# A second level of the seven-product form in the down product of a gated FFN with a long convolution

## The chip, the cores and the metric

The kernel runs on one core of one Trainium2 chip. The metric is the device time of one execution in microseconds. A core has the engines TensorE (PE, matrix products, with its weight loads shown apart as PEld), VectorE (DVE), ScalarE (ACT), GpSimd (POOL) and SyncE (SP). In this kernel SP and POOL mainly issue DMA transfers; the transfers themselves are done by 16 DMA engines of the core.

## The reference, cut to what matters

For 2048 tokens of 1024 features the reference computes, in float32,

```python
xn = layernorm(x)
y  = causal_convolution(xn, K) + D[0] * xn       # along the 1024 features, K (1024 entries) from the S4 parameters
h  = silu(xn @ Wg.T) * (xn @ Wu.T)               # 2752 inner entries, int4 weights, groups of 64
out = x + y + h @ Wd.T                           # Wd int4 as well, 1024 x 2752
```

Two products dominate: gate and up (2048 x 1024 by 1024 x 5504) and down (2048 x 2752 by 2752 x 1024). The convolution runs along each token's 1024 features and is a triangular Toeplitz product. The int4 weights have to be unpacked, scaled and shifted before use.

## The kernel before

A float32 product is made of three float16 products: each operand is split into a hi and a lo float16 part (hi is a rounded copy, made on ACT; lo is operand minus hi, made on DVE), and hi·hi + hi·lo + lo·hi is summed in PSUM. So each 128 x 128 weight block costs three weight loads and three matmuls (the loops over `PASS`).

Both large products use one level of the Winograd form of the 2 x 2 block product: seven block products P1 to P7 of sums of blocks (factors) in place of eight. `PROD` names, for each product, the factor of either side.

Phase A makes gate and up for 21 i tiles of 128 inner entries (and a half tile), j = 0 to 20, over two pairs of token chunks (`cp` = 0, 1; a chunk is 512 tokens). For each j, `load_w` (L351) turns two packed granules into split factors: `unpack` on DVE, 16 scaling ACTIVATEs on ACT, four sums on DVE, a hi copy on ACT, a lo subtraction on DVE (`factors`, L305), and a transposing DMA into a `wf` tile. `gate_up` (L411) then issues 84 matmuls and its evacuations. `finish_h` (L465) waits for two i tiles, forms the seven sums of h, splits each into hi and lo, and stores them to DRAM (`HSP`). Beside this, at ten values of j (`WD_AT`, L45), `load_wd` (L366) unpacks two granules of the down weights, forms and splits the seven factors and stores them (`WDN`). At six further places `keep_x` stores blocks of x for the convolution, and L507 to L624 compute the convolution's kernel.

Phase B makes the down product over ten pairs of i tiles. For each of the two `cp` and seven products, `load_factor` (L823) brings split factors back, weights through a transposing DMA (`wd`) and h plainly (`hd`), all through the SP queue. `product` (L844) issues 30 matmuls of 512 columns per 128 tokens: h is the stationary operand, the weights the moving one. `rest` (L854) adds, in the same PSUM bank, the convolution and the last one and a half i tiles; `common` (L879) makes a part of the convolution in another bank. `finish` (L888) loads x, adds the partial results to it on DVE and stores the output. The sums U2 and U3 are kept in `h` tiles of 512 columns.

What sets the order: every engine runs its instructions in one fixed order, written when the kernel is built. Only the first part of phase A (L630 to L699) and the steps around `pinned` have an order written by hand. Elsewhere the framework's scheduler orders them by program priority and its own timeline (L1044). A tile that reuses a buffer makes its first writer wait for the last user. So a DMA issued by SP or POOL that waits for a buffer, or for data, holds up all that stands behind it in that queue.

The tile pools that matter here: `u8` (14 buffers of 8 KB per partition for x blocks, inputs, and later `wd` and `hd`), `h` (10 of 2 KB), `hf` (3), `nat` (2), `wf` (4), the dequantized granule `w` (2), and 8 PSUM banks.

## Time and profile before

| | |
|---|---|
| three runs | 1349.52, 1351.09, 1357.06 us; median 1351.09 us |
| profiled execution | span 1353.8 us. Of the three times shown only 1357.06 us is not below that span, so only that one can be the profiled execution's own; 3.3 us would then lie around the span |
| TensorE busy | 1304.3 us, 96% of the span, granted clock 0.991 |
| VectorE, ScalarE, GpSimd busy | 791.9 us (58%), 630.2 us (47%), 211.8 us (16%) |
| phase A on TensorE | until 856.5 us |
| phase B on TensorE | 856.5 to 1350.1 us: 1680 matmuls of `product`, and 832 of `rest` and `common` |
| DMA | 242.7 MB, 179 GB/s over the span; 65% of the DMA engines' time on SP's queues, 4.5% on POOL's |

How to read it: busy time is the union of an engine's instruction spans. Matmuls are pipelined, so the mean of one (380 ns for 512 columns) is a latency; what a matmul costs in a stream is the distance between starts. An idle time is put down to the event that ended it. Most vector and scalar instructions carry the line of a helper (L79 or L84), so groups are told apart by the names of their operands. A DMA's time to landing counts from its issue.

### The profile page before, as it was taken

The page shows a single profiled execution, that of the slowest core. Times are in us where ns is not written, and L with a number is a line of the kernel's source. Part 1 is how long each engine was busy: PE and PEld are TensorE (multiplying, and loading weights), DVE is VectorE, ACT ScalarE, POOL GpSimd, SP SyncE. Part 2 cuts the span into 40 slices and gives each one's busy share as a digit, 9 for nine tenths or more (in the row PEclk, how much of TensorE's full clock was granted, in tenths as well). Part 3 has the DMA queues.
Part 4 walks back from the last instruction along what each step waited for, and adds up shares of the span by engine and source line. Part 5 has one row for each costly group of instructions (what it writes and reads, how often), then busy time and mean ns, then how long its engine had stood idle before and what let it go on. Part 6 is the DMA issues. An engine that isn't in the chain of part 4 may idle for free.

```text
span 1353.8 us, 17402 instructions
## 1 busy us (share of the span) xinstructions
PE 1304.3 (96%) x6404; PEld 614.2 (45%) x6404; DVE 791.9 (58%) x1303; ACT 630.2 (47%) x1374; POOL 211.8 (16%) x354
## 2 busy tenths in 40 slices
PE   2798999999999999999999999989999999999998
PEld 2343444444444444444444444434444554444464
DVE  7679998788798878997887865241111412111131
ACT  5478378697896676879988872100000000000000
POOL 5235042221321121212242300000000000000000
PEclk9899999999999999999999999999999999999999
DMA  8994728557466656665866668999878759767420
GB/s 228 232 199 107 171 68 188 128 144 191 122 183 155 183 166 159 198 192 170 211 177 158 176 124 227 264 305 268 203 199 220 225 176 255 199 162 203 124 86 24
DMA packets 400370, 242.70 MB, mean 179 GB/s; under 512 B 338132, under 2 KB 358556, under 8 KB 396444
## 3 DMA queue, kind: packets, MB, share of 16 engines
q1 hardware_dynamic: 394012, 225.98, 64.7%
q0 software_dynamic: 6272, 15.60, 4.5%
q8 instruction: 50, 0.82, 0.2%
q14 instruction: 36, 0.29, 0.1%
HBM read 83.47 MB, written 74.45 MB: 117 GB/s over the span
## 4 chain that ended last, share of the span: by engine, by line
PE 64%; DMA 4%; DVE 2%; SPq 1%; issue 1%; ACT 1%; DVEq 0%; ACTq 0%
PE o L848 25%; PE C L418 9%; PE D L418 9%; PE A L418 8%; PE B L418 4%; PE o L876 4%; PE o L859 2%; DMA wf<-nat 2%; SPq L79 1%; DMA hd<-HSP 1%; PE o L867 1%; PE c L884 1%; PE o L871 1%; PE o L861 1%; PE o L860 1%
## 5 line engine op out<-in xcount | busy, mean ns | idle before, releaser
L418 PEld LDWEIGHTS <-wf 128*128 128x128 f16 x3192 | 312.8, 98 | 386.4 <-issue 11.8
L848 PE MATMUL o<-wd,hd 128*128 128x512 f16 x1680 | 368.3, 380 | 4.0 <-DMA hd<-HSP 4.0
L79 ACT ACTIVATE w<-w,sc 128x64 f32<-128x64 int32 x960 | 326.8, 427 | 65.3 <-DVE w L79 62.6
L848 PEld LDWEIGHTS <-hd 128*128 128x128 f16 x1680 | 163.7, 98 | 197.5 <-DMA hd<-HSP 4.5
L418 PE MATMUL C<-x,wf 128*128 128x512 f16 x912 | 211.9, 382 | 3.7 <-DVE u L79 3.7
L418 PE MATMUL A<-x,wf 128*128 128x512 f16 x912 | 211.3, 380 | 3.0 <-DMA wf<-nat 2.4
L418 PE MATMUL D<-x,wf 128*128 128x512 f16 x912 | 209.2, 379 | 0.0
L79 DVE TENSOR_TENSOR nat<-w,nat 128x1792 f16<-128x1792 f32 x58 | 117.0, 2019 | 24.4 <-ACT nat L79 24.2
L79 ACT COPY v<-o 128x512 f32<-128x512 f32 x8 | 4.7, 585 | 268.5 <-PE o L848 268.5
L79 DVE TENSOR_TENSOR w<-w 128x256 f32<-128x256 f32 x232 | 97.0, 419 | 48.5 <-ACT w L79 46.4
L79 ACT CAST nat<-w 128x1792 f16<-128x1792 f32 x58 | 97.3, 1678 | 35.0 <-DMA wf<-nat 29.2
L418 PE MATMUL B<-x,wf 128*128 128x512 f16 x456 | 107.5, 382 | 0.0
L390 PEld LDWEIGHTS <-wf 128*128 128x128 f16 x624 | 56.7, 104 | 91.3 <-DMA wf<-natp 30.5
L79 DVE TENSOR_TENSOR v<-o,v 128x512 f32<-128x512 f32 x24 | 16.6, 691 | 138.8 <-PE o L848 138.8
L79 DVE SCALAR_TENSOR_TENSOR o<-o,o 128x512 f32<-128x512 f32 x32 | 22.0, 688 | 125.5 <-PE o L876 125.3
L283 POOL TENSOR_SCALAR sc<-sz 128x16 f32<-128x16 f32 x61 | 49.0, 803 | 233.8 <-ACT w L79 225.2
L255 POOL DMA_DIRECT2D raw<-in_raw x56 | 32.5, 581 | 267.2 <-DVE w L79 252.5
L390 PE MATMUL g<-x,wf 128*128 128x512 f16 (+1 forms) x264 | 48.1, 341 | 27.2 <-DMA wf<-natp 24.9
L79 DVE SCALAR_TENSOR_TENSOR o<-v,o 128x512 f32<-128x512 f32 x32 | 21.9, 691 | 77.3 <-DMA o<-in_x 57.7
L876 PE MATMUL o<-band,xc 128*128 128x512 f16 (+3 forms) x384 | 57.5, 300 | 0.0
L79 DVE TENSOR_TENSOR hf<-ha,hf 128x512 f16<-128x512 f32 x72 | 48.9, 685 | 13.3 <-ACT hf L79 13.2
L79 ACT CAST hf<-ha 128x512 f16<-128x512 f32 x72 | 43.5, 612 | 23.5 <-DVE ha L79 18.0
(132 smaller groups left out, 1097.9 us busy)
## 6 DMA issues: line engine op xcount, KB each, us to landing
HSP<-hf SPq DMA_DIRECT2D x60, 512.0 KB, 3.6
hd<-HSP SPq DMA_DIRECT2D x28, 768.0 KB, 5.3
WDN<-nat SPq DMA_DIRECT2D x20, 896.0 KB, 4.6
raw<-in_raw POOLq DMA_DIRECT2D x56, 256.0 KB, 4.1
hd<-HSP SPq DMA_DIRECT2D x14, 1024.0 KB, 5.6
n<-in_xp SPq DMA_DIRECT2D x16, 512.0 KB, 4.8
XSP<-x SPq DMA_DIRECT2D x8, 1024.0 KB, 5.8
xc<-XSP SPq DMA_DIRECT2D x8, 1024.0 KB, 7.1
```

Of the source, the lines that this page charges most:

```text
L79: return method(*args, **kw)
L255: ld.dma_start(raw, raw_d[gi].rearrange("p (a b) -> p a b", a=16))
L283: G.tensor_scalar(sc[:, 0], sz[:, 0], WS, None, ALU.mult)
L390: PE.matmul(ps[:, ts], w(k, wi), xt[k // 4][:, xi, k % 4, ts], start=(k == 0 and n == 0), stop=(k == 7 and n == 2))
L418: PE.matmul(ps, wf[kt // 2][:, 4 * fa + 2 * wi + kt % 2, :], xt[:, xi, kt, :], start=(start and kt == 0 and n == 0), stop=(stop and kt == ...
L848: PE.matmul(ps.rearrange("p (a b) -> p a b", a=2), hh[gi][:, n, hi, q * P : (q + 1) * P], wd[gi][:, n, :, wi, :], start=(g0 + n == 0 and k ...
L859: PE.matmul(ps, hpl[:, c, hi, ts], wp[:, 0, wi, cols], start=False, stop=False, skip_group_check=again)
L860: PE.matmul(ps, hpl[:, c, 2, ts], wp[:, 1, 0, cols], start=False, stop=False, skip_group_check=again)
L861: PE.matmul(ps, hpl[0:64, c, 2, ts], wp[0:64, 1, 1, cols], start=False, stop=False, skip_group_check=again)
L867: PE.matmul(ps[:, 0:256], xt[:, xi, k + 2, ts], diff[:, bi, P - P * k : P - P * k + 256], start=False, stop=False, skip_group_check=again)
L871: PE.matmul(ps[:, 256:512], xt[:, xi, k, ts], diff[:, bi, 512 - P * k : 768 - P * k], start=False, stop=False, skip_group_check=again)
L876: PE.matmul(ps[:, P * k : 512], xt[:, xi, k, ts], band[:, bi, 0 : 512 - P * k], start=False, stop=(k == 3 and n == 2), skip_group_check=again)
```

## The change

The down product gets a second level of the same form. Each of the seven outer products (k) is itself a 2 x 2 block product, over the token halves (`cp`), the two halves of the ten pairs of i tiles, and alternate tiles of 128 hidden entries; it is made of seven inner products (m). An inner product is 60 matmuls of 256 columns: two halves `qq` of 256 tokens, two tiles of 128 tokens, five pairs of i tiles, three passes. The 49 items (k, m) follow one another, with the next k's first item moved ahead of the last two of this k.

In phase A, `finish_h` stores the seven sums of h unsplit as float32 (`HF`), one DMA each. `load_wd` handles two granules from the two halves of the pairs at once, makes the second-level factors (four more subtractions on half tiles), and stores each of the seven inner factors of either kind apart (`WD2`). Only one of the four blocks of x is stored for the convolution; the other three stay in SBUF.

In the last phase, `load_a` brings h sums back through POOL's queue, `operands` makes the second-level sums of h on DVE and splits them on ACT and DVE (`gsplit`), and `load_b` brings the weights through a transposing DMA on SP. `prepare` runs four items ahead; there are five `g` buffers and five for b. Accumulators U and W stay in SBUF. `result` loads a partial output through POOL, adds to it and stores it.

The convolution and the last i tiles become a stage between the two (`conv`), with PSUM banks of their own. Its sum with x goes to DRAM (`PART`), and `result` reads it back. `add_split` makes its hi copy on ACT rather than DVE. The pools are laid out anew: x blocks live in `ux` (6) and `ut` (8, shared with the inputs), `h` has 12 buffers, and the pools of the last phase take the place of those of phase A tile by tile.

```diff
-        u8 = pool("u8", bufs=14)
-        hp_ = pool("h", bufs=10)
-        hfp = pool("hf", bufs=3)
+        hp_ = pool("h", bufs=12)
...
-        XSP = [[dr.tile([P, 2, 4, 512], F16, name=f"XSP{c}{f}") for f in range(4)] for c in range(2)]
-        HSP = [dr.tile([7, P, NPAIR, 1024], F16, name=f"HSP{c}") for c in range(2)]
+        XSP = [dr.tile([P, 2, 4, 512], F16, name=f"XSP{c}") for c in range(2)]
...
-        WDN = dr.tile([7, P, NPAIR, 1024], F16, name="WDN")
+        WD2 = [dr.tile([7, P, NPAIR // 2, 2, 2, P], F16, name=f"WD{m}") for m in range(1, 8)]
+        PART = [[dr.tile([1024, 512], F32, name=f"PART{c}{h}") for h in range(2)] for c in range(2)]
...
+        ea = ExitStack()
+        right = lambda name, **k: ea.enter_context(tc.tile_pool(name=name, side="right", **k))
+        uxp = pool("ux", bufs=6, side="right")
+        utp = right("ut", bufs=8)
+        wfp = right("wf", bufs=4)
+        natp = right("nat", bufs=2)
+        dqp = right("dq", bufs=2)
+        early = ExitStack()
+        left = ExitStack()
+        right2 = lambda name, **k: left.enter_context(tc.tile_pool(name=name, reuse_waits="tile", **k))
+        hfp = early.enter_context(tc.tile_pool(name="hf", bufs=2))
...
+                home, tag = (uxp, "ux") if f in (0, 1, 3) else (utp, "ut")
+                xf[cp, f] = home.tile([P, 2, 4, 512], F16, tag=tag, name=f"x{cp}_{f}")
...
-            def load_wd(p):
+            def load_wd(u):
+                pr, kq = divmod(u, 2)
+                gs = [G_WD + 2 * p + kq for p in (pr, pr + NPAIR // 2)]
+                ws = []
+                for gi, home in zip(gs, (wxp, dqp)):
+                    w = dequant(gi, home=home)
+                    sums(w, True)
+                    ws.append(w.rearrange("p f (m c) -> p f m c", m=2))
+                wa, wb = ws
+                tt, sub = V.tensor_tensor, ALU.subtract
+                def put(w, ms, products):
+                    nat = natp.tile([P, 7, 2, 2, P], F16, tag="nat", name=f"nd{u}_{products[0]}")
+                    split(nat[:, :, ms].rearrange("p f m a c -> p a f m c"), w[:, :, ms])
+                    for m, i in zip(range(2)[ms], products):
+                        SP.dma_start(
+                            WD2[i - 1][:, :, pr, kq].rearrange("f p a c -> p f (a c)"),
+                            nat[:, :, m].rearrange("p f a c -> p f (a c)"),
+                        )
+                put(wa, slice(0, 1), (1,))
+                tt(wa[:, :, 0], wa[:, :, 1], wa[:, :, 0], sub)
+                tt(wa[:, :, 1], wb[:, :, 1], wa[:, :, 1], sub)
+                put(wb, slice(0, 2), (2, 3))
+                tt(wb[:, :, 1], wb[:, :, 1], wa[:, :, 0], sub)
+                tt(wb[:, :, 0], wb[:, :, 0], wb[:, :, 1], sub)
+                put(wa, slice(0, 2), (5, 7))
+                put(wb, slice(0, 2), (4, 6))
...
-                def emit(f0, srcs):
-                    pc = piece(f"hf{nm}_{f0}")
-                    for i, s in enumerate(srcs):
-                        split(pc[:, i], s)
-                    n = len(srcs)
-                    SP.dma_start(
-                        HSP[cp][f0 : f0 + n, :, pr, :].rearrange("f p c -> p f c"),
-                        pc[:, :n].rearrange("p f a b -> p f (a b)"),
-                    )
-                emit(0, (s0, s1))
...
+                def emit(f, src):
+                    SP.dma_start(HF[cp][f, :, j // 2, :], src)
+                s4, s5, s6 = (htile(f"s{n}_{nm}") for n in (4, 5, 6))
+                emit(0, s0)
+                emit(1, s1)
+                emit(3, s3)
                 V.tensor_tensor(s4, s0, s2, ALU.subtract)
+                emit(4, s4)
                 V.tensor_tensor(s2, s2, s3, ALU.add)
-                V.tensor_tensor(s0, s2, s0, ALU.subtract)
-                V.tensor_tensor(s1, s1, s0, ALU.subtract)
-                emit(5, (s0, s1))
-                emit(2, (s2, s3))
...
+                V.tensor_tensor(s5, s2, s0, ALU.subtract)
+                emit(5, s5)
+                V.tensor_tensor(s6, s1, s5, ALU.subtract)
+                emit(6, s6)
...
+            early.close()
+            wxp = right2("wx", bufs=1)
...
-                if j in XS_AT:
-                    keep_x(*divmod(XS_ORDER[j - XS_AT[0]], 4))
...
+        poolb = lambda name, **k: es.enter_context(tc.tile_pool(name=name, reuse_waits="tile", **k))
+        fp = poolb("f", bufs=6, side="right")
+        gp = poolb("g", bufs=5, side="right")
+        bep = poolb("be", bufs=3, side="right")
+        cvp = poolb("cv", bufs=1)
+        half = NPAIR // 2
...
+        def gtile(name):
+            return gp.tile([P, half, 2, 512], F16, tag="g", name=name)
+        def load_a(k, r, c):
+            t = fp.tile([P, half, 512], F32, tag="f", name=f"a{k}_{r}{c}")
+            G.dma_start(t, HF[r][PROD[k][0], :, half * c : half * c + half, :])
+            fac[r, c] = t
...
+        def load_b(k, m, n):
+            home, tag = (bep, "be") if n % 5 < 3 else (uxp, "ux")
+            t = home.tile([P, half, 2, 2, P], F16, tag=tag, name=f"b{k}_{m}")
+            SP.dma_start_transpose(
+                t.rearrange("p a b c d -> p (a b c) d"), WD2[m - 1][PROD[k][1]].rearrange("p a b c d -> p (a b c d)")
+            )
+            return t
+        def gsplit(src, name):
+            g = gtile(name)
+            A.copy(g[:, :, 0], src)
+            V.tensor_tensor(g[:, :, 1], src, g[:, :, 0], ALU.subtract)
+            return g
+        def operands(k, m, n):
+            tt, sub, add = V.tensor_tensor, ALU.subtract, ALU.add
+            if m == 1:
+                load_a(k, 0, 0)
+                src = fac[0, 0]
+            elif m == 2:
+                load_a(k, 0, 1)
+                src = fac[0, 1]
+            elif m == 6:
+                load_a(k, 1, 0)
+                load_a(k, 1, 1)
+                s1 = fac["s1"] = fp.tile([P, half, 512], F32, tag="f", name=f"s{k}")
+                tt(s1, fac[1, 0], fac[1, 1], add)
+                tt(fac[1, 0], fac[0, 0], fac[1, 0], sub)
+                tt(fac[0, 0], s1, fac[0, 0], sub)
+                fac["s2"] = src = fac[0, 0]
+                fac["s3"] = fac[1, 0]
+                fac["a12"], fac["a22"] = fac[0, 1], fac[1, 1]
+            elif m == 5:
+                src = fac["s1"]
+            elif m == 7:
+                src = fac["s3"]
+            elif m == 4:
+                src = fac["a22"]
+            else:
+                src = fac["a12"]
+                tt(src, src, fac["s2"], sub)
+            b = load_b(k, m, n)
+            return gsplit(src, f"g{k}_{m}"), b
...
+        def conv(cp, c, hh, hpl, xc, xs):
+            for q in range(4):
+                ts = slice(q * P, (q + 1) * P)
+                cols = slice(512 * hh, 512 * hh + 512)
+                ps = bank(f"cv{cp}{c}{hh}{q}")
...
+                for hi, wi in PASS:
+                    mm(ps, hpl[:, c, hi, ts], wp[:, 0, wi, cols])
+                mm(ps, hpl[:, c, 2, ts], wp[:, 1, 0, cols])
+                mm(ps, hpl[0:64, c, 2, ts], wp[0:64, 1, 1, cols], stop=True)
+                t0 = 1024 * cp + 512 * c + P * q
+                o = htile(f"p{cp}{c}{hh}{q}")
+                SP.dma_start(o, x[t0 : t0 + P, cols])
+                V.scalar_tensor_tensor(o, ps, osc, o, ALU.mult, ALU.add)
+                if hh:
...
+                SP.dma_start(PART[cp][hh][512 * c + P * q : 512 * c + P * q + P, :], o)
+        items = [(k, m) for k in SEQ for m in (1, 2, 6, 5, 7, 4, 3)]
+        for n in range(0, len(items) - 7, 7):
+            items[n + 5 : n + 8] = [items[n + 7]] + items[n + 5 : n + 7]
+        ready = []
+        def prepare():
+            n = len(ready)
+            if n < len(items):
+                ready.append(operands(*items[n], n))
...
+        for cp in range(2):
+            hpl = gp.tile([P, 2, 3, 512], F16, tag="g", name=f"hpl{cp}")
             SP.dma_start(hpl, HPL[cp])
-            xc = []
+            x7 = fp.tile([P, 2, 4, 512], F16, tag="f", name=f"x7_{cp}")
+            SP.dma_start(x7, XSP[cp])
+            xc = [xf[cp, 3], xf[cp, 1], x7, xf[cp, 0]]
+            xs = fp.tile([P, 2, 2, 2, 512], F16, tag="f", name=f"xs{cp}")
...
-                wd, hh = load_factor(cp, i)
...
-                    product(ps, wd, hh, q, i not in REST or i == 5)
-                    if i in REST and i != 5:
-                        rest(ps, hpl, xc, *REST[i], q)
...
+            for c, hh in ((0, 0), (1, 0), (0, 1), (1, 1)):
+                conv(cp, c, hh, hpl, xc, xs)
+                if cp:
+                    prepare()
...
+        U = [uxp.tile([P, 4, 512], F32, tag="ux", name=f"U{cp}") for cp in range(2)]
+        W = [uxp.tile([P, 4, 512], F32, tag="ux", name=f"W{cp}") for cp in range(2)]
...
+        banks, zs = {}, {}
+        def matmuls(k, m, qq):
+            g, b = ops
+            new = m in (1, 2, 5)
+            key = {1: "A", 6: "A", 7: "A", 4: "A", 2: "E", 5: "D", 3: "D"}[m]
+            if new:
+                banks[k, key, qq] = bank(f"{key}{k}_{qq}")
+            ps = banks[k, key, qq]
+            for q in range(2):
+                dst = ps[:, 256 * q : 256 * q + 256].rearrange("p (a b) -> p a b", a=2)
+                ts = slice(256 * qq + P * q, 256 * qq + P * q + P)
+                for i in range(half):
+                    for n, (hi, wi) in enumerate(PASS):
+                        PE.matmul(dst, g[:, i, hi, ts], b[:, i, :, wi, :],
+                                  start=(new and q + i + n == 0), stop=(q == 1 and i == half - 1 and n == 2),
+                                  skip_group_check=True)
...
+            tt, add = V.tensor_tensor, ALU.add
+            if k == 1 and z is None:
+                A.copy(view(U, blk, qq), ps)
+                return
+            if k in (1, 6):
+                tt(view(U, blk, qq), ps, z, add)
+            elif k == 7:
+                tt(view(W, blk, qq), ps, z, add)
...
+                for q in range(2):
+                    G.dma_start(o[:, q], pv[:, q])
+                if k == 5:
+                    u = view(U, blk, qq)
+                    tt(u, ps, z, add)
+                    V.scalar_tensor_tensor(o, u, osc, o, ALU.mult, ALU.add)
+                    w = view(W, blk, qq)
+                    V.scalar_tensor_tensor(o, w, osc, o, ALU.mult, ALU.add)
+                else:
+                    u = temp(f"x{k}_{blk}{qq}")
+                    tt(u, ps, z, add)
+                    V.scalar_tensor_tensor(o, u, osc, o, ALU.mult, ALU.add)
+                    if k == 4:
+                        w = view(W, blk, qq)
+                        tt(w, w, view(U, blk, qq), ALU.subtract)
+                for q in range(2):
+                    SP.dma_start(ov[:, q], o[:, q])
...
+        def evacuate(k, m, qq, ps):
+            src = {1: None, 4: W}.get(k, U)
+            if m == 5:
+                return
+            if m in (1, 6, 7):
+                blk = {1: 11, 6: 12, 7: 22}[m]
+                z = zs[k, blk, qq] = temp(f"z{k}_{blk}{qq}")
+                if src is None:
+                    A.copy(z, ps)
+                else:
+                    V.tensor_tensor(z, ps, view(src, blk, qq), ALU.add)
+                if m == 7:
+                    evacuate(k, "57", qq, banks[k, "D", qq].rearrange("p (q k c) -> p q k c", q=2, k=2))
+            else:
+                blk = {2: 11, "57": 22, 3: 12, 4: 21}[m]
+                if m == 4:
+                    z = view(src, blk, qq) if src is not None else None
+                else:
+                    z = zs.pop((k, blk, qq))
+                result(k, blk, qq, ps, z)
+        for n, (k, m) in enumerate(items):
+            prepare()
+            ops = ready[n]
+            for qq in range(2):
+                evacuate(k, m, qq, matmuls(k, m, qq))
```

## Prediction

> **What bounds the kernel now.** I read the page's shares first, then the stages, then TensorE's timeline, then the groups and waits of the engine that gets new work.
>
> ```profile
> span 1353.8 us, 17402 instructions
> PE 1304.3 (96%) x6404; PEld 614.2 (45%) x6404; DVE 791.9 (58%) x1303; ACT 630.2 (47%) x1374; POOL 211.8 (16%) x354
> ...
> PE   2798999999999999999999999989999999999998
> ...
> DVE  7679998788798878997887865241111412111131
> ACT  5478378697896676879988872100000000000000
> ...
> DMA  8994728557466656665866668999878759767420
> ```
>
> TensorE is full in all but the first two slices; DVE and ACT are loaded for 25 slices and nearly idle after. The windows put numbers on that (columns: stretch, length, busy PE, PEld, DVE, ACT, POOL, clock, DMA share, GB/s):
>
> ```profile
> 376.00:412.50 36.50, 35.12 (x164) 16.01 (x163) 34.03 (x65) 31.38 (x79) 9.82 (x20) 1.00 0.73 188
> 815.00:900.00 85.00, 80.97 (x372) 36.36 (x371) 38.66 (x66) 13.50 (x23) 0.00 (x0) 0.98 1.00 272
> 856.50:1353.80 497.30, 489.53 (x2514) 239.22 (x2511) 99.25 (x158) 5.93 (x10) 0.00 (x0) 1.00 0.73 192
> ```
>
> The last phase has 398 us of free DVE time. Phase A has little: one i tile is 36.5 us of TensorE, and DVE is at 34.0 in the worst such window. TensorE's timeline gives the price of 256 columns, each matmul with its own weight load:
>
> ```profile
> 1335.59 0.83 PE L867 MATMUL o<-diff,xc 128*128 128x256 f16 x6
> 1336.25 0.82 PE L871 MATMUL o<-diff,xc 128*128 128x256 f16 x6
> 1336.91 1.79 PE L876 MATMUL o<-band,xc 128*128 128x512 f16 x12
> 1338.54 0.82 PE L884 MATMUL c<-band,xs 128*128 128x256 f16 x6
> 1339.19 6.64 PE L848 MATMUL o<-wd,hd 128*128 128x512 f16 x30
> 1345.67 0.81 PE L859 MATMUL o<-wp,hpl 128*128 128x512 f16 x3
> ```
>
> Starts are what counts: six of 256 columns take 0.66, 0.66 and 0.65 us (110 and 108 ns each), thirty of 512 take 6.48 us (216 ns). Halving the columns halves the time. The groups of DVE and ACT (busy, mean ns):
>
> ```profile
> L79 DVE TENSOR_TENSOR nat<-w,nat 128x1792 f16<-128x1792 f32 x58 | 117.0, 2019 | 24.4 <-ACT nat L79 24.2
> L79 ACT CAST nat<-w 128x1792 f16<-128x1792 f32 x58 | 97.3, 1678 | 35.0 <-DMA wf<-nat 29.2
> L79 DVE TENSOR_TENSOR hf<-ha,hf 128x512 f16<-128x512 f32 x72 | 48.9, 685 | 13.3 <-ACT hf L79 13.2
> ```
>
> In a stream DVE's starts are closer than its durations: 0.60 us apart at 512 entries, 1.13 at 1024 (timeline, 161 to 178 us). So 0.53 us per further 512: 1.93 at 1792, 2.72 at 2560, 1.0 at 896. Last a wait and three DMA rows (KB each, us to landing):
>
> ```profile
> DVE o L79 <- DMA o<-in_x: 57.7, 13, 10.7
> ```
> ```profile
> raw<-in_raw POOLq DMA_DIRECT2D x56, 256.0 KB, 4.1
> raw<-in_raw SPq DMA_DIRECT2D x9, 256.0 KB, 4.0
> wd<-WDN SPq DMA_TRANSPOSE x42, 7.9
> ```
>
> **The down product on TensorE.** Removed: 56 runs of 30 matmuls, 56 x 6.48 = 362.9 us. Added: 49 items x 60 = 2940 matmuls of 256 columns at 109 ns, 320.5 us (317.5 at 108, 323.4 at 110). Net **-42.4 us** (-45.4 to -39.5). TensorE sets the end, so all of it counts as long as the operands arrive.
>
> **The convolution as a stage.** The matmuls are the same. In the chain, a tile's share is the pitch of two runs of `product` less one run: 9.39 - 6.47 = 2.92 us with 17 matmuls (hidden half 0), 11.36 - 6.47 = 4.89 with 35; 16 x 2.92 + 16 x 4.89 = 125 us, moved. Its evacuations, 48 DVE operations x 0.60 = 29 us, and its 32 stores lie beside these 125 us; without that cover they would cost 29. `add_split` on ACT is hidden: ACT is free there. Entry: today 1350.1 - 856.5 = 493.6 us hold 362.9 + 125, so 5.7 us are idle, 4.0 of them for `hd`. The new entry finds x block 3 in SBUF, but `wp` and `hpl` need memory that phase A's weight tiles leave late: between nothing and 13.3 us (8.6 for `wp` and 4.7 for `hpl` to land, one after the other), net -6 to +8. I take 0, nearest today's gap.
>
> **Start of the second level.** The convolution's x7 and sums hold two of six `f` buffers until its last matmul, four loads of h hold the rest, so s1 waits. From then: three sums 3 x 2.72 = 8.2, the ACT copy of 2560 entries 2.3 (1.68 at 1792 plus 768 x 0.83 ns), the lo part 2.7: 13.2 us, plus the last evacuations 1.2. Two ready items cover 2 x 60 x 0.109 = 13.1. I take **+3** (0 if sums come early, 13 if no item is ready).
>
> **Steady state: DVE.** Per k seven splits and four sums of 2560 entries: 77 x 2.72 = 209 us. Evacuations: 69 DVE operations for each `qq` (3, 11, 7, 7, 15, 15, 11 over the k's order), 138 x 0.60 = 83 us. Before the last item can start at 48 x 6.54 = 314 us, DVE owes 75 x 2.72 + 130 x 0.60 = 282 us: 90%. For k = 4 and 5 it is 29.9 + 18 = 48 us against 45.8; the four items of lead (26 us) cover that. In fourteen i tile windows of phase A (266 to 778 us) DVE ran at 75 to 93%, mean 83%. At 93% the 282 us fit; at 85% they take 332, 18 too long. I take **+8**, between; bounds 0 and 34 (81%). A late operand stops TensorE at once, since matmuls stay in order; a late evacuation has one item, 6.5 us, before its bank is needed.
>
> **Queues in that stage.** SP: 49 transposes of 2560 columns; `wd` issues take 5.6 us at the median for 3413 columns on average, so 4.2 x 49 = 206 us, and 64 stores x 0.4 = 26: 232 of 321 us. Behind a store that waits for DVE stand the next transposes; the lead covers 26 us of that. POOL: 28 loads of h and 64 of `PART` at about 0.6 us, 55 us. Bytes: 32 MB transposed, 37 MB of h, 17 MB of `PART` and output, less 7 loaded ahead: 79 MB in 321 us, 246 GB/s, under the 272 that the window at 815 us shows. No charge; a shortfall shows in the rivals.
>
> Here a rule speaks against the change. The Trainium skill (SBUF — State Buffer, section "SBUF: two separate sides") says that a DMA issued from POOL stalls while DVE runs an operation that takes both ports, since its descriptors can't be written. The trace: raw granules of 256 KB landed after 4.1 us from POOL and 4.0 from SP, while DVE was about 83% busy. By a figure of that page (620 ns becoming 3100), an estimate of 64 late `PART` loads would add 159 us of waiting and make the kernel slower; by the rows it adds nothing. I go by the rows.
>
> **Phase A.** `finish_h` drops 140 splits (the `hf` groups): 94 us of DVE and 83 of ACT. `load_wd` adds 40 subtractions of 896 (40 us) and, ten times, splits of 3.5 instead of 2 granule sizes: +29 us of DVE, +25 of ACT. So DVE gets 25 us less and ACT 58 us less over 19 i tiles. But the new work is bunched: an i tile with `load_wd` gets 7 us of DVE and loses 5, and 34.0 becomes 36, the whole tile. It also keeps a `w` tile of the gate work for longer and passes four `nat` tiles where two went. SP: 60 more stores of h and 50 more of weights at 0.38 us, 6 fewer of x: +39 us over 700, beside a queue that mostly waits. h tiles now live until their store lands (7 at once; 12 buffers). The inputs have 8 buffers rather than 14 shared ones; the late ones wait for normalised tiles, off TensorE's path. Bounds: -7 (the idle of the windows 320 to 480 and 640 to 800 us goes) and +24 (each `load_wd` makes one `wf` late by 2.4 us, the wait of TensorE for `wf` today). I take **+3**: average load falls, bunching rises.
>
> **Tail.** Today 3.7 us after the last matmul; then 0.69 + 0.69 + 3.1 for the store: **+1** (0 to 2).
>
> **Sum.** -42.4 + 0 + 3 + 8 + 3 + 1 = -27.4. The profiled span of 1353.8 becomes 1326.4, and 1329.7 with the 3.3 us around it. That execution, if it is the 1357.06 one, lies 6 us above the median of the runs; on the median 1351.09 the forecast is **1323.7 us**.
>
> **Rivals.** Half a percent (6.8 us) is about what a measurement can tell from no change: 1344 to 1358.
> - *All of it arrives* (0.08): no stall at all, 1351.1 - 42.4 = 1308.7; at the cheaper column 1305.7. For it: TensorE kept full with DVE at 93%. Against: nowhere did DVE hold 90% for 300 us.
> - *DVE becomes the bound, no change* (0.12): at 80% the 282 us take 353, 39 too long: -42.4 + 39 + 3 + 3 + 1 = +3.6, 1354.7. For it: ACT to DVE hand-overs already cost DVE 24 us at `nat`. Against: there is a lead of four items.
> - *Slower: partial outputs come late* (0.14). The `PART` loads share POOL's queue, in order, with loads of h that wait for an `f` buffer; DVE then waits inside `result`, with the next operands behind it. Today's like wait, `o` for x, is 57.7 / 13 = 4.4 us, free since DVE is idle. 32 results x 4.4 = 141 us; three in four, 106, less 32 us of spare DVE time: +74, so 1351.1 - 42.4 + 74 + 7 = 1390. It decides from 67 us, 2.1 us per result. Against: buffers of s1 and s3 come free three or more items ahead.
> - *Slower: phase A stalls* (0.08). Four `nat` tiles per `load_wd` delay the gate weights. ACT's longest wait for `nat` today is 6.8 us; ten of them give 68 for my 3: 1389. It decides at 2.4 us each.
>
> **Chances.** My forecast (1312 to 1344) has 0.58. Faster: 0.58 + 0.08 = 0.66; same: 0.12; slower: 0.14 + 0.08 = 0.22. The range 1304 to 1375 leaves out most of the slow rivals' far ends.
>
> **What would show it.** Right: TensorE's new matmuls 0.65 us per six; DVE about 90% busy for 320 us; few microseconds of TensorE idle put down to `g`; phase A ending within 5 us of 856.5. Wrong: DVE idle before `o` on POOL's DMA, TensorE idle on `b` (SP held up) or on `wf`, or a 256-column pitch above 0.115 us, each 0.01 us costing 29 us.

## The result, and the profile after

The changed kernel is slower: the ratio of its times to those of the kernel before is 1.048 (95% interval 1.042 to 1.054). The forecast was 1323.7 us; the profiled execution of the changed kernel took 1420.74 us, its span is 1419.0 us. (Single executions of it took 1411.57 to 1448.78 us; the ratio leaves disturbed ones out.)

The stages, cut at the first and last start of each stage's matmuls, in microseconds of the two profiled executions:

| | before | predicted change | after | change |
|---|---|---|---|---|
| phase A, end | 856.5 | +3 | 913.6 | +57.1 |
| convolution with its entry | 125 + 5.7, mixed with the product | 0 | 143.5 | +12.8 |
| down product: columns | 362.9 | -42.4 | 320.5 | -42.4 |
| down product: start and stalls | in the 5.7 above | +11 | 356.7 - 320.5 | +36.2 |
| after the last matmul | 3.7 | +1 | 5.2 | +1.5 |
| sum | 1353.8 | -27.4 | 1419.0 | +65.2 |

From the page of the changed kernel: span, busy time, the 40 slices, and the two large DMA queues (q1 is SP's, q0 POOL's).

```profile
span 1419.0 us, 20450 instructions
PE 1288.2 (91%) x7664; PEld 742.4 (52%) x7664; DVE 1039.9 (73%) x1372; ACT 700.7 (49%) x1313; POOL 239.3 (17%) x446
...
PE   3799999989978998999879979959999998998898
...
DVE  7679977678777877879777854536249696697795
...
DMA  9994627675747576467677637486529999999997
...
q1 hardware_dynamic: 432508, 194.27, 59.4%
q0 software_dynamic: 13376, 60.70, 15.0%
```

TensorE's row has holes all along, where the row before had nines. Its busy time fell by 16 us, not by 42, and its idle time rose from 49.5 us to 130.8. The DMA row is at nine for all of the last stage but its last slice. TensorE's waits (us in total, times, longest):

```profile
PE A L449 <- ACT u L79: 45.0, 9, 8.7
PE A L989 <- DVE z L79: 25.0, 11, 6.1
PE g L421 <- DMA wf<-natp: 24.5, 3, 21.4
PE cv L907 <- DMA hpl<-HPL: 14.6, 1, 14.6
```

Of these four the kernel before had two, as follows; it had no wait for `hpl`, and no `z`:

```profile
PE g L390 <- DMA wf<-natp: 24.9, 3, 21.4
PE A L418 <- ACT u L79: 0.6, 1, 0.6
```

So only the wait for `wf` was there at this size before; the other three came with the change. They lie in three stages: phase A, the last stage, and the convolution's entry.

**Phase A.** First its sum, in windows that end with phase A, before and after (length, busy PE, PEld, DVE, ACT, POOL, granted clock, DMA share, GB/s):

```profile
0.00:856.50 856.50, 814.81 (x3892) 374.95 (x3893) 692.62 (x1146) 624.29 (x1364) 211.76 (x354) 0.99 0.68 172
0.00:913.60 913.60, 827.68 (x3892) 376.32 (x3893) 687.11 (x1068) 575.86 (x1243) 179.54 (x355) 0.97 0.67 167
```

For the same 3892 matmuls TensorE is idle 44 us longer and busy 13 us longer, at a lower clock: together the 57 us. VectorE and ScalarE have less to do than before. Now one of the nine waits, in the timeline (start, length, instruction, idle time before it and what ended it). First ScalarE, then TensorE:

```profile
699.55 1.67 ACT L79 CAST nd<-w 128x1792 f16<-128x1792 f32 x1
706.39 1.69 ACT L79 CAST nd<-w 128x1792 f16<-128x1792 f32 x1 [5.17 <-DVE w L79]
707.98 3.75 ACT L79 ACTIVATE w<-w,sc 128x64 f32<-128x64 int32 x11
711.63 0.56 ACT L79 COPY u<-A 128x512 f32<-128x512 f32 x1
```
```profile
701.10 2.75 PE L449 MATMUL D<-x,wf 128*128 128x512 f16 x12
712.25 7.70 PE L449 MATMUL A<-x,wf 128*128 128x512 f16 x22 [8.39 <-ACT u L79]
719.78 2.54 PE L449 MATMUL C<-x,wf 128*128 128x512 f16 x11
```

`gate_up` copies bank A to `u2` on ScalarE before TensorE may add product 2 to that bank. The copy stands behind a cast of `load_wd` that waits 5.17 us for VectorE's chain of subtractions, behind the cast itself, and behind eleven scalings. TensorE's three products of lead are used up, and it stops for 8.39 us. Then the 22 matmuls take 7.53 us to the next start; at the pitch of 0.216 us they take 4.75. Windows of 1 us show why (the granted clock is the third number from the end):

```profile
714.00:715.00 1.00, 1.00 (x4) 0.34 (x3) 1.00 (x2) 1.00 (x3) 0.00 (x0) 0.50 0.95 223
717.00:718.00 1.00, 1.00 (x4) 0.33 (x3) 0.97 (x4) 1.00 (x4) 0.64 (x2) 0.53 0.00 0
718.00:719.00 1.00, 1.00 (x6) 0.47 (x5) 0.38 (x1) 1.00 (x5) 1.00 (x2) 1.00 0.00 0
```

For some 5.7 us after the stall the clock is at 0.50. So this stall costs 2.8 us more than its idle time. The Trainium skill (TensorE: Matmul & The Clock Gate, "Part 1: The HAM clock gate (the "warmup" mystery)") has the rule: after an idle window of about 3.4 us the array gets half its clock, until it has been busy for a while. The rows of this stall agree. But a shorter one did it too: in the kernel before, TensorE waited 2.44 us for `wf` until 786.25 us, and from 788 to 790 us the clock was at 0.50. So 3.4 us is no safe limit.

**The last stage.** Windows of 60 us (busy PE, PEld, DVE, ACT, POOL, granted clock, DMA share, GB/s):

```profile
1060.00:1120.00 60.00, 60.00 (x551) 53.60 (x550) 56.97 (x31) 31.60 (x20) 6.67 (x11) 1.00 1.06 268
1120.00:1180.00 60.00, 55.31 (x488) 48.21 (x487) 40.64 (x30) 18.61 (x8) 10.14 (x16) 0.97 1.12 196
1180.00:1240.00 60.00, 53.36 (x471) 46.71 (x469) 43.37 (x29) 18.61 (x8) 2.61 (x5) 0.94 1.03 202
```

For the first 60 us TensorE is full, with DVE at 57 of 60. Then the DMA engines are as busy as in that first window but move a quarter less. VectorE's and GpSimd's waits in that stage:

```profile
DVE o L79 <- DMA o<-PART: 40.6, 5, 10.7
DVE s L79 <- DMA a<-HF: 12.0, 2, 11.3
```
```profile
POOL a L821 <- DVE g L79: 213.6, 22, 30.2
...
POOL o L1020 <- DMA out<-o: 36.6, 3, 17.6
```

VectorE stands in `result` until a partial output has landed, and an evacuation `z` that TensorE needs stands behind it. Three things could make the partial outputs late: loads of h ahead of them in GpSimd's queue, buffers that come free only when a store has left SyncE's queue, or the DMA engines themselves.

### The profile page after: what moved, and what is told of

Same layout as the page of the kernel before. It is cut to its first block, busy times and chain, and to the rows that moved or that the text cites. A ratio compares the mean times of both kernels' runs of the same rounds, so it can differ in the third digit from the quotient of the medians.

```text
span 1419.0 us, 20450 instructions
## 1 busy us (share of the span) xinstructions
PE 1288.2 (91%) x7664; PEld 742.4 (52%) x7664; DVE 1039.9 (73%) x1372; ACT 700.7 (49%) x1313; POOL 239.3 (17%) x446
## 3 DMA queue, kind: packets, MB, share of 16 engines
q1 hardware_dynamic: 432508, 194.27, 59.4%
## 4 chain that ended last, share of the span: by engine, by line
issue 20%; DVE 12%; PE 10%; DMA 7%; ACT 6%; POOL 1%; DVEq 0%; SPq 0%; POOLq 0%; ACTq 0%
ACT w L79 4%; DMA o<-PART 4%; PE A L449 3%; DVE g L79 3%; PE C L449 3%; PE D L449 2%; DMA a<-HF 2%; DVE a L79 1%; DMA out<-o 1%; DMA wf<-nat 1%; DVE o L79 1%; PE A L989 1%; PE B L449 1%; DVE z L79 1%; DVE w L79 1%
## 5 line engine op out<-in xcount | busy, mean ns | idle before, releaser
L79 ACT ACTIVATE w<-w,sc 128x64 f32<-128x64 int32 x960 | 325.9, 428 | 58.7 <-DVE w L79 56.5
L989 PEld LDWEIGHTS <-g 128*128 128x128 f16 x2940 | 291.1, 99 | 65.6 <-issue 27.9
L449 PE MATMUL A<-x,wf 128*128 128x512 f16 x912 | 224.7, 398 | 46.4 <-ACT u L79 45.0
L989 PE MATMUL A<-b,g 128*128 128x256 f16 x1680 | 195.6, 280 | 25.1 <-DVE z L79 25.0
L79 ACT CAST g<-a 128x2560 f16<-128x2560 f32 x42 | 97.5, 2326 | 198.3 <-DVE a L79 68.8
L79 DVE TENSOR_TENSOR w<-w 128x256 f32<-128x256 f32 (+1 forms) x252 | 118.8, 473 | 52.3 <-ACT w L79 49.5
L79 DVE TENSOR_TENSOR g<-a,g 128x2560 f16<-128x2560 f32 x42 | 118.1, 2817 | 4.6 <-ACT g L79 4.6
L989 PE MATMUL D<-b,g 128*128 128x256 f16 x840 | 94.2, 273 | 0.3 <-DMA b<-WD 0.3
L79 ACT CAST nd<-w 128x1792 f16<-128x1792 f32 (+1 forms) x40 | 59.3, 1494 | 64.9 <-DMA wf<-nat 33.7
L79 DVE TENSOR_TENSOR nat<-w,nat 128x1792 f16<-128x1792 f32 x38 | 76.8, 2020 | 18.5 <-ACT nat L79 18.5
L79 DVE TENSOR_TENSOR nd<-w,nd 128x1792 f16<-128x1792 f32 (+1 forms) x40 | 71.3, 1789 | 20.2 <-ACT nd L79 20.2
L907 PEld LDWEIGHTS <-x 128*128 128x128 f16 x576 | 52.3, 98 | 23.1 <-issue 2.0
```

The costliest lines, as they stand in the source:

```text
L79: return method(*args, **kw)
L449: PE.matmul(ps, wf[kt // 2][:, 4 * fa + 2 * wi + kt % 2, :], xt[:, xi, kt, :], start=(start and kt == 0 and n == 0), stop=(stop and kt == ...
L907: PE.matmul(dst, w, m, start=first[0], stop=stop, skip_group_check=True)
L989: PE.matmul(dst, g[:, i, hi, ts], b[:, i, :, wi, :], start=(new and q + i + n == 0), stop=(q == 1 and i == half - 1 and n == 2), skip_grou ...
```

## The experiments

Unless it says otherwise, a run has one profiled execution. Phase A's end is from here on the last start of its matmuls: 856.4 us before the change, 913.4 after it. In the eight kernels that leave phase A as it is (the changed one and seven below) it lies between 908.9 and 915.5 us, so some 7 us there are no effect.

### Phase A: how much is the new work, and how much its order

The second level left out of `load_wd`: no subtractions, two splits instead of four, the same stores.

```diff
-                put(wa, slice(0, 1), (1,))
-                tt(wa[:, :, 0], wa[:, :, 1], wa[:, :, 0], sub)
...
+                for w, (i1, i2), more in ((wa, (1, 2), (5, 7)), (wb, (3, 4), (6,))):
...
```

> Leaves out the second level of the down weights in phase A: no further subtractions, two splits of 1792 entries per pair of granules in place of 3.5, the same seven stores (so the result is not the reference's). Theory A, the splits and subtractions of load_wd hold up the copy of bank A in ScalarE's queue: TensorE's idle time before A on ScalarE's u falls from 45 us to under 10, and phase A ends at 865 us or earlier in place of 914. Rival B, the h tiles that wait for their stores hold it up: the idle time stays above 35 us and phase A ends after 900. The last stage is the same in both, some 357 us.

Phase A ended at 869.9 us: without the second level's work in it some 44 of the 57 us are gone. The wait for `u` fell from 45.0 to 12.2 us. Both miss what was expected (865 and 10 us) by a little. But the total stayed at 1423.49 us, because the last stage, where nothing was edited, took 404.6 us. There TensorE waited for weights:

```profile
PE D L978 <- DMA b<-WD: 35.6, 2, 20.2
PE A L978 <- DMA b<-WD: 23.4, 2, 16.8
PE E L978 <- DMA b<-WD: 12.9, 1, 12.9
```

So the last stage isn't stable: in the other runs below that left it alone it took 357 to 375 us. An edit of that stage is read as an effect only if its time lies outside 357 to 405 us.

Six of the seven stores of h left out (`emit(1, s1)` to `emit(6, s6)` removed, the loads reading factor 0):

> Leaves out six of the seven stores of h for each pair of i tiles and reads the first sum in place of each (so the result is not the reference's). Rival B, h tiles held by their stores: phase A ends before 880 us in place of 914 and TensorE's idle time before A falls by more than 30 us. Theory A, side work on ScalarE: phase A ends within 8 us of 914, with 35 us or more of that idle time.

Phase A ended at 904.9 us, the total was 1411.8. That is outside both expectations, but near theory A: the stores of h are worth some 9 us at most, and the wait for `u` was still 32.1 us.

The hi casts of `load_wd` on VectorE instead of ScalarE:

```diff
-                    split(nat[:, :, ms].rearrange("p f m a c -> p a f m c"), w[:, :, ms])
+                    d = nat[:, :, ms].rearrange("p f m a c -> p a f m c")
+                    V.tensor_copy(d[:, 0], w[:, :, ms])
+                    V.tensor_tensor(d[:, 1], w[:, :, ms], d[:, 0], ALU.subtract)
```

> The hi parts of the second-level down weights are made on VectorE rather than ScalarE, nothing is left out. Theory A: ScalarE no longer waits for VectorE in the middle of load_wd, so TensorE's idle time before A falls from 45 to 20 us or less and phase A ends at 890 us or earlier. If VectorE is the limit in those i tiles instead (it gets some 40 us more work over ten i tiles), phase A ends later than 914.

Phase A ended at 912.7 us, no effect and neither of the two expectations; the total was 1419.26. TensorE still waited 33.8 us for ScalarE's `u`. ScalarE had less to do and waited more: for VectorE's `u` 99.2 us (47.4 after the change), for its `w` 87.2 (56.5).

```profile
ACT u L79 <- DVE u L79: 99.2, 17, 13.5
ACT w L79 <- DVE w L79: 87.2, 21, 10.3
```

So ScalarE's load alone isn't it: the copy of `u` stands behind whatever ScalarE waits for.

The ten weight steps at other rows:

```diff
-WD_AT = (5, 6, 7, 9, 11, 13, 14, 15, 16, 17)
+WD_AT = (4, 6, 8, 10, 12, 14, 16, 17, 18, 19)
```

> Nothing is left out: load_wd comes after i tiles 4, 6, 8, 10, 12, 14, 16, 17, 18, 19 in place of 5, 6, 7, 9, 11, 13 to 17. Theory G, the work of load_wd is too much where i tiles with it follow one another: TensorE's idle time before A on u falls from 45 to 20 us or less and phase A ends at 890 us or earlier. Theory A in its stricter form, each load_wd holds up ScalarE's queue once wherever it stands: idle stays at 35 us or more and phase A ends after 905.

Phase A ended at 897.2 us, 16 earlier and between the two expectations, with 20.3 us of waits for `u`. The last stage took 373.8, and the total, 1421.13, did not move.

The copy of `u` on VectorE:

```diff
-                A.copy(u2, bA)
+                V.tensor_copy(u2, bA)
```

> Edit: in the last phase A products, the copy of the first product's bank (tile u) is made by VectorE instead of ScalarE; nothing else changes. Order theory: TensorE's 45.0 us of waits for ScalarE's copy come from the copy standing behind ScalarE's casts and scalings of the down weights, which wait for VectorE; on VectorE the copy stands behind other work, most of the waits go, phase A (913.6 us) ends near 875 to 885, and the total is 1382 to 1395. Latency rival: VectorE waits for ScalarE in the same chains, so the waits come back as TensorE waiting for VectorE's copy, phase A ends at 905 to 920 and the total stays within 10 us of 1420.

Phase A ended at 880.6 us: 33 us for one line that takes no work away and gives the busier engine more. TensorE's waits:

```profile
PE A L449 <- DVE u L79: 16.4, 6, 5.3
PE A L449 <- DMA wf<-nat: 6.4, 4, 2.9
```

The order theory held for phase A; the total, 1405.8, missed its 1382 to 1395 because the last stage took 374.6 us. So 33 of the 57 us hang on the place of that copy in ScalarE's queue. They aren't beside the 44 us of the first run but largely the same: the second level's work is what the copy stood behind.

### The last stage: queue, buffer, or DMA engines

The partial outputs not read back (64 loads less, 8.4 MB):

```diff
-                for q in range(2):
-                    G.dma_start(o[:, q], pv[:, q])
...
-                    V.scalar_tensor_tensor(o, u, osc, o, ALU.mult, ALU.add)
+                    V.scalar_tensor_tensor(o, u, osc, u, ALU.mult, ALU.add)
...
```

> The last stage does not read the partial output back (the output lacks x and the convolution); VectorE has the same number of operations. Theory C, VectorE waits for partial outputs that stand behind 1.3 MB loads of h in POOL's DMA queue: VectorE's wait for o (41 us) is gone, TensorE waits less than 8 us for VectorE in that stage and the stage takes 335 us or less in place of 357. Rival D, VectorE's own work is the limit: the stage stays above 350 us and TensorE still waits 20 us for z. Rival E, the 16 DMA engines are the limit as a whole: the stage shortens to about 345 with waits for b or a instead. Phase A as in the changed kernel.

The last stage took 329.5 us instead of 356.7, the total was 1393.61: the loads of partial outputs and the waits for them are worth 27 us. The edit takes away 8.4 MB of transfers too, so it doesn't say whether their lateness comes from a queue or from the DMA engines.

Their loads on ScalarE's queue, apart from the loads of h:

```diff
-                    G.dma_start(o[:, q], pv[:, q])
+                    A.dma_start(o[:, q], pv[:, q])
```

> Nothing is left out: the 64 loads of partial outputs are issued by ScalarE's DMA queue in place of POOL's. Theory C, the loads are late because their data stands behind 1.3 MB loads of h in one queue: VectorE's wait for o falls from 41 to under 10 us, and the last stage from 357 to 338 us or less. Theory E, the DMA engines as a whole are the limit: the wait stays above 25 us and the stage above 350.

And the other way round, the loads of h on ScalarE's queue:

```diff
-            G.dma_start(t, HF[r][PROD[k][0], :, half * c : half * c + half, :])
+            A.dma_start(t, HF[r][PROD[k][0], :, half * c : half * c + half, :])
```

> Nothing is left out: the 28 loads of h are issued by ScalarE's DMA queue in place of POOL's, the partial outputs stay with POOL. Theory C: as with the partial outputs moved, the stage takes 338 us or less. Theory F, transfers of POOL's queue make the transposing loads of the second-level weights slow: the DMA share of the stage falls under 0.9 as well and the median transposing issue from 4.1 us to near the 2.6 us minimum. Theory E: no change.

Neither was faster: last stages of 376.3 and 378.9 us, within the range of kernels that left the stage alone, and totals of 1436.34 and 1438.55. VectorE's waits in the first and the second of them:

```profile
DVE s L79 <- DMA a<-HF: 25.4, 2, 13.2
DVE o L79 <- DMA o<-PART: 22.1, 3, 14.4
DVE o L79 <- DMA out<-o: 21.0, 1, 21.0
```
```profile
DVE s L79 <- DMA a<-HF: 28.6, 2, 22.7
DVE o L79 <- DMA o<-PART: 23.6, 3, 20.0
```

With the two kinds of load in separate queues, both are late. So the sharing of GpSimd's queue alone isn't the cause. Nor is it that GpSimd issues them, as the rule weighed in the prediction would have it: from ScalarE's queue the loads of h landed after 9.2 us at the median, from GpSimd's after 8.6. Partial outputs issued by GpSimd landed after 7.1 us in the changed kernel, and after 4.3 in the run with h in SyncE's queue below.

Four buffers of their own for the partial outputs, in the space of the convolution's band:

```diff
+        conv_only.close()
+        olp = poolb("ol", bufs=4)
...
-                o = temp(f"o{k}_{blk}{qq}")
+                o = olp.tile([P, 512], F32, tag="ol", name=f"o{k}_{blk}{qq}")
...
```

> Edit: the tiles that take the stored partial outputs get four buffers of their own, in the space that the convolution's band leaves free; in the changed kernel they share twelve with all other temporaries. Buffer theory: GpSimd's partial output loads are issued late because a buffer comes free only when an output store has gone, and the stores stand in SyncE's queue behind transposing loads (GpSimd waited 36.6 us for stores); then VectorE's wait for partial outputs (40.6 us) falls below 15 us, the last stage from 356.7 us to 332 to 342, the total to about 1400. Rival, the DMA engines as a whole are the limit: the wait stays at 30 us or more, or moves to the first-level activations, and the last stage stays at 350 or more.

The last stage took 366.7 us, the total was 1427.34. VectorE waited as long as before and GpSimd longer, so the buffer theory, as stated, fell:

```profile
DVE o L79 <- DMA o<-PART: 39.4, 3, 26.1
```
```profile
POOL o L1024 <- DMA out<-o: 121.5, 13, 27.0
```

The loads of h on SyncE's queue, in one line with the transposing loads of the weights:

```diff
-            G.dma_start(t, HF[r][PROD[k][0], :, half * c : half * c + half, :])
+            SP.dma_start(t, HF[r][PROD[k][0], :, half * c : half * c + half, :])
```

> Edit: the 28 loads of the stored activations in the last stage are issued on SyncE's queue, where the transposing loads of the weights are, instead of GpSimd's. Theory that two queues hinder each other: the transposing loads and the large loads then alternate instead of running side by side, the busy share of the DMA engines falls from about 1.0 to below 0.9 at the same 200 GB/s, and the last stage from 356.7 us to 335 to 345. Rival: the bytes and the order of the queue decide; each activation load then waits behind transposing loads for up to 30 us and the last stage is 360 to 400 us.

The last stage took 329.8 us, the total was 1392.82. Its windows:

```profile
1060.00:1120.00 60.00, 60.00 (x552) 53.68 (x550) 57.31 (x32) 31.01 (x19) 2.88 (x4) 1.00 1.03 272
1120.00:1180.00 60.00, 60.00 (x552) 53.77 (x551) 54.63 (x38) 20.93 (x9) 5.75 (x8) 1.00 1.07 254
1180.00:1240.00 60.00, 60.00 (x552) 53.78 (x550) 55.16 (x39) 21.43 (x10) 4.31 (x6) 1.00 0.87 212
```

TensorE is full for 240 us, and of VectorE's waits the one for partial outputs is gone. The expectation was right on the direction, a little short on the time (335 to 345 us), and wrong on the share: it stayed near 1, and the bytes went up (254 GB/s instead of 196 in the second window).

The weights loaded without transposing them, which makes the product wrong and leaves only its times to read:

```diff
-            SP.dma_start_transpose(
-                t.rearrange("p a b c d -> p (a b c) d"), WD2[m - 1][PROD[k][1]].rearrange("p a b c d -> p (a b c d)")
-            )
+            SP.dma_start(t, WD2[m - 1][PROD[k][1]])
```

> Edit: the 49 loads of the second-level weights in the last stage fetch the same bytes without transposing them, so the output of the down product is wrong and only the times are of use. Theory that the transposing loads fill the DMA engines: the busy share in the last stage falls from about 1.0 to 0.6 or less, the partial outputs and activations land sooner, VectorE's waits for them (52.6 us together) fall below 15 us, and the last stage goes from 356.7 us to 325 to 335. Rival, the waits come from the order of queues and buffers and not from the engines' load: stores still leave in order, but the waits stay above 30 us and the last stage at 345 or more.

The last stage took 320.9 us, the 320.5 of its columns with no stall at all; the total was 1379.18.

```profile
1120.00:1180.00 60.00, 60.00 (x552) 53.78 (x550) 58.60 (x40) 20.93 (x9) 11.19 (x17) 1.00 0.77 265
1180.00:1240.00 60.00, 60.00 (x552) 53.78 (x551) 53.11 (x37) 20.94 (x9) 4.65 (x8) 1.00 0.60 216
```

The share fell to 0.77 and 0.60 and VectorE waited 2.7 us for partial outputs.

The time of the packets on the DMA engines, from the queues' shares of the span, all for the same 256 MB: (59.4 + 15.0)% of 1419.0 = 1056 us after the change; 65.6% of 1377.4 = 904 without transposing; 72.5% of 1391.0 = 1008 with h in SyncE's queue, and 1008 to 1024 in the six kernels that have it there, this one and the combinations below. So the 49 transposing loads add 150 us or more of packet time on all 16 engines over plain ones. But this time is no fixed price: in the seven kernels that left this stage's queues as they are it goes from 1053 to 1103 us, and most where the last stage is longest (1103 us in the run with 404.6). The two runs with a third queue, 75.2% and 75.3% or 1079 and 1082 us, lie inside that spread, so a price of the third queue isn't shown. The Trainium skill (DMA: Bandwidth & Descriptors, "Queues, rings and completion order") says that an engine goes round its queues packet by packet; that fits late landings on both queues, but no run here shows the packets' order. That h in SyncE's queue removes most of the stalls, and plain loads of the weights all of them, is shown; why the mixture costs more inside the engines is not.

### The entry of the convolution

The loads of x kept behind the reload of the last hidden tile in SyncE's queue:

```diff
-                SP.dma_start(o, x[t0 : t0 + P, cols])
+                with tc.issue_after(hld.ins):
+                    SP.dma_start(o, x[t0 : t0 + P, cols])
...
```

> Nothing is left out: the loads of x of the convolution stage stand behind the load of hpl in SP's queue in place of ahead of it. If hpl is late because SP waits 19 us for a free h tile with wp and hpl behind that load, TensorE's wait for hpl falls from 14.6 us to under 5 and the convolution stage from 143.5 to 134 us or less. If wp waits for its memory until phase A's last matmuls, the wait stays at 12 us or more.

The wait for `hpl` went from 14.6 to 11.6 us, the total was 1427.54. The 19 us that the loads of x took in the queue were mostly not the reason.

### The causes together

The loads of h on SyncE's queue and the copy of `u` on VectorE, both:

> Edit: the two single edits that helped, together: the last stage's activation loads on SyncE's queue, and the copy of tile u on VectorE. If the stall of phase A (ScalarE's order, 33 us by its run) and that of the last stage (two DMA queues side by side, 27 us by its run) are separate, the times add: phase A ends near 880, the last stage lasts about 330 us, the total is 1355 to 1368, still slower than before. If they share a cause, so that one comes back when the other goes (for instance because phase A's stores then meet the loads differently), the total stays above 1378.

1357.82 us, ratio to before 1.003 (1.001 to 1.005). Phase A ended at 881.8 us and the last stage took 332.6: the two add up, so they are separate causes.

With that, the band products of two column halves issued ahead of those that need the reloaded tile:

```diff
-            for c, hh in ((0, 0), (1, 0), (0, 1), (1, 1)):
-                conv(cp, c, hh, hpl, xc, xs)
...
+                    both = [conv_x(cp, c, hh, xc) for hh in range(2)]
+                    for hh in range(2):
+                        conv_h(cp, c, hh, hpl, xc, xs, hld, both[hh])
...
```

> Edit: as the run with both edits, and the entry of the convolution is reordered: for the first column half the band products of eight units are issued before the products that need the reloaded last hidden tile, and the loads of x wait until that tile's load has been issued. Theory: TensorE's wait of 14 to 17 us for that tile is covered by 17.9 us of band products (an estimate from their columns at the pitch of the profile), so the convolution stage takes 126 to 134 us instead of 143 and the total is 10 to 18 us under the run with both edits, 1340 to 1356. Rival: the tile's load is late by as much as the stage starts earlier, because the memory that it goes to is freed by phase A's last weight tile; then the stage stays at 138 or more.

1351.69 us, ratio 0.998 (0.996 to 1.000). The convolution stage took 134.4 us against 141.2, at the edge of the expectation; 6.6 us of the wait are left:

```profile
PE cv L928 <- DMA hpl<-HPL: 6.6, 1, 6.6
```

With the spread weight steps as well:

> Edit: as the run with the reordered convolution entry, and the ten second-level weight steps are put at rows 4, 6, 8, 10, 12, 14, 16, 17, 18, 19 instead of 5, 6, 7, 9, 11, 13 to 17. Theory: with the copy of u on VectorE the steps that follow one another directly still stall phase A; spreading them brought 16 us by itself, at most 10 of them are left here: phase A ends at 870 to 880, the total is 1332 to 1352 and no longer distinguishable from before (1350) or below it. Rival: the stalls that spreading removed are the ones that the copy on VectorE already removed; phase A ends at 880 or later and the total is that of the run with the reordered entry within 4 us.

1354.09 us, ratio 0.999 (0.997 to 1.001). Phase A ended at 874.7 us instead of 882.2, as expected, but the wait for `hpl` grew to 13.2: TensorE came earlier to a tile that did not. The total missed its 1332 to 1352 by a little.

Then the stores of the last hidden tile on GpSimd's queue, without and with the spread steps:

```diff
-                    SP.dma_start(HPL[cp][:, :, 0:2, :], pc)
+                    G.dma_start(HPL[cp][:, :, 0:2, :], pc)
```

> Edit: as the run with the reordered convolution entry, and the two stores of the last hidden tile are issued by GpSimd instead of SyncE. There SyncE issued the transposing load of wp only at 897.85 us, though phase A's last product ended at 882.2, because the store of the last hidden tile stood before it in SyncE's queue and waited for VectorE until 894.8. Theory: wp is then loaded while the tile is still made, the tile's reload is issued about 4 us earlier, TensorE's wait of 6.6 us falls to 0 to 3, the convolution stage from 134.4 us to 127 to 131, the total is 3 to 8 us lower: 1344 to 1349, the interval of the ratio to before wholly below 1. Rival: wp waits for memory and not for the queue; the wait stays at 5 us or more and the total within 2 us of 1352.

> Edit: as the run before it (stores of the last hidden tile on GpSimd), with the spread weight steps as well. In the run with spread steps phase A ended 7.5 us earlier (874.7 against 882.2) but the wait at the convolution's entry was 6.6 us longer (13.2 against 6.6), so nothing was left. Theory: that wait was the same queue order, so the gain now stays and the total is 4 to 8 us under that of the run before it, 1337 to 1345. Rival: the entry is bound by the last hidden tile itself, which VectorE finishes at 887 to 894 whatever TensorE does; the wait stays above 8 us and the total is within 2 us of the run before it.

1351.66 us (ratio 0.998, 0.996 to 1.000) and 1351.43 us (0.998, 0.996 to 1.000): nothing gained, the rivals held. The wait was 7.3 and 13.8 us. SyncE's queue in the first of them:

```profile
867.20 5.50 SPq L79 DMA_DIRECT2D x<-XSP  x2
895.77 4.58 SPq L79 DMA_TRANSPOSE wp<-WPN  x1
900.45 0.52 SPq L79 DMA_DIRECT2D hpl<-HPL  x1
```

The queue was empty from 872.7 us, and `wp` still went out only at 895.77, 3.3 us after GpSimd had issued the tile's store (892.5), about what such a store takes to land. So `wp` waits for memory, as the rival said; that it is the memory of the stored tile itself is inferred from this time alone.

One rival stayed untested. In the changed kernel VectorE began on the last hidden tile's second half of tokens at 911.25 us and ended with the subtraction that started at 925.24, without a pause; in between it also ran the convolution's sums of x and of the band. Had the tile's operations gone first, its store could have left earlier. No run moved them.

The best of these versions stand level with the kernel before; none beats it by the half percent that a measurement can tell.

## Why the prediction was wrong, step by step

- **The down product on TensorE, -42.4: right.** With the operands there in time the last stage took 320.9 us (weights not transposed) against the computed 320.5.
- **Phase A, +3: mis-sized, +57.1.** The step saw that work would be bunched and that average load would fall, and went mainly by the average. It bounded the loss by the wait for `wf`, 2.4 us in each of ten steps. That wait stayed small (1.3 us in all); what came was a wait for `u`, in nine places of up to 8.7 us, the longer ones with slow matmuls behind them, for which the sum had no term (13 us). The failed step is the choice of row: it asked who needs the new work's result, and not what stands behind its waits in ScalarE's queue. The copy that frees TensorE's bank stood there, and moving it alone gave 33 us back. The load also fell by less than the prediction counted: over phase A VectorE's busy time by 6 us, not 25, and ScalarE's by 48, not 58.
- **The rival "phase A stalls": its place, not its mechanism.** It priced ScalarE waiting for `nat` buffers that delay the gate weights. The loss (57) was near its 68 by luck, through another tile.
- **The convolution's entry, 0 with bounds -6 to +8: outside its bounds, +12.8.** It counted two landings one after the other and took the nearest old gap. The reload of the last hidden tile, and by the inference above `wp` too, starts only when that tile has been made and stored, and its evacuation chain ends some 12 us after phase A's last matmul (882.2 to 894.8 us in the run with reordered entry).
- **Start of the second level, +3: nothing.** Between the convolution and the first item there is no gap, and TensorE is full for the first 60 us.
- **Steady state, DVE, +8: the wrong resource.** VectorE kept pace wherever its data were there: 57 of 60 us in the first window, and no stall in the run without transposing.
- **Queues in that stage, no charge: the step that failed in the last stage.** 79 MB were set against 272 GB/s, a rate from a window in which one queue carried transposing and plain transfers in line (99.9% of the DMA time) and no other queue ran beside it. In the new stage a second queue ran beside the transposing loads, and after its first 60 us the engines delivered about 200 GB/s at a share of 1. A queue's bytes were counted, the mixture's price was not. Start and steady state together were put at +11; they cost 36.2. With h in SyncE's queue 9.3 of the 36.2 were left, without transposing 0.4.
- **The rival "partial outputs come late": right in the symptom.** VectorE waited for `PART` in `result`, 40.6 us in all, and without those loads the stage was 27 us shorter. Its reason, the loads of h ahead in GpSimd's queue, fell: separate queues did not help. So did its price, 4.4 us in three of four results: the profile has five waits of about 8 us.
- **Tail, +1: right (+1.5).**
- **The sum.** 57.1 - 3 = 54.1 from phase A, 36.2 - 11 = 25.2 from the last stage, 12.8 from the entry and 0.5 from the tail: the 92.6 us between -27.4 and +65.2. The two slow rivals were given chances as alternatives; what they named, stalls in both stages, came in both, though not for their reasons, and the range had no case for their sum. The 3.3 us that the prediction put round the span don't fit the changed kernel, where they are 1.7 (1420.74 less 1419.0); the forecast doesn't rest on them.

What stays open: with all edits phase A still ends 18 to 26 us later than before (874.7 to 882.2), part of it waits for VectorE's `u`; and why the untouched last stage took between 357 and 405 us in different kernels.

## What to carry to other kernels

When work is added to an in-order engine, list what stands behind its waits in that queue and how much lead the receiver has, above all copies that free a matmul bank: busy time fell here on both side engines and the stage grew by 57 us. Price a DMA-bound stage by a row that has the same mixture of queues and transposing loads, not by the best rate elsewhere. When several stalls are possible in different stages they add, so the slow end of a range needs the case in which all of them come.

## What was unexpected of the hardware

- The price of the slow clock after a stall: the `A` group of phase A was busy 224.7 us for the same 912 matmuls that took 211.3 before. In the kernel before a wait of 2.44 us was enough for half the clock.
- The DMA engines showed a busy share (the packets' times added up, so it can pass 1) of 0.95 to 1.12 while they moved 196 to 217 GB/s, and 0.77 at 265 GB/s with the weights not transposed. A share near 1 does not say that no more bytes can be moved: with h in SyncE's queue they moved 254 at 1.07.
- A transposing load of the second-level weights (640 KB) took 7.5 us to land at the median and up to 27.2 in the changed kernel; not transposed it took 4.5.
